# Staging an image's output as two column halves and spreading its stores

## The chip, the cores and the metric

The kernel runs on one core of one Trainium2 chip. The core has a matrix engine (TensorE, PE in the profile), a vector engine (VectorE, DVE), a scalar engine (ScalarE, ACT), GpSimd (POOL) and SyncE (SP), which here only issues transfers. Transfers between device memory and the on-chip memory run on 16 DMA engines, whoever issues them. The metric is the device time of one execution in microseconds, as the median of several runs.

## The reference

The input `x` has 16 images of 64 channels, 128 x 128 pixels, float32. Layer 0 is a spectral convolution: a Hartley transform, a product over channels for the 20 x 20 lowest modes, the inverse transform, a Gaussian blur along all four axes (also batch and channel), and a mask that keeps the columns 0 to 32 and 96 to 127. Layer 1 is a small network on top:

```
h    = afno(group_norm(x)) + x          # spectral mixing of 32 x 32 modes, two small complex layers
feats = gelu(fe_w @ group_norm(h))
out  = mean over 2 shared of gelu(shared_w[s] @ feats)
gate = softmax of the 4 best of 16 expert scores, from the mean of feats, one set per image
out += sum over the 4 chosen experts of gate[e] * gelu(expert_w[e] @ feats)
out += h
```

All products with 64 x 64 weights are per pixel. The output has the size of the input, 4.19 MB per image.

## The kernel before

The first stages transform all images to modes, mix channels, and run the spectral layer; they leave per image 1 MB of column spectra in device memory (`bmd`), further mode tables (`od`, `obd`, `ond`) and a small edge correction (`ehd`). The change doesn't touch them, apart from tables that depend on the order of tiles.

The last stage makes the output, image after image. An image's pixels lie in eight tiles `t` of 16 columns each; the tuple `TILES` (line 32) says which columns the tile `t` holds. A tile has 128 partitions (64 channels times two halves of the rows) and 1024 elements each, so that one matmul group, one Gelu and one vector operation handle it.

The work of an image is cut in pieces (`PIECES`, line 965), each with places counted in groups from the image's first group; an image has `NG` = 48 groups, and all pieces of all images are sorted by place (line 978). The pieces are:

- `spectrum` (line 698), at -84 and -76: SyncE loads the edge correction and four 256 KB slices of `bmd` into the tile `bm`, and then four loads from `od`, `obd`, `ond`. There is one `bm`; a load into it has to wait until TensorE has read the image before.
- `columns` (710), `pixels` (724) and `feature` (796): inverse transforms on TensorE, evacuated by ScalarE (tiles in `BY_ACT`) or VectorE; `pixels` adds the edge correction to the first rows of the tiles that hold columns with a mask of one; `feature` is the first Gelu layer.
- `gate` (816), in eight steps at -3 to 15: the expert scores; its seventh step, at group 12, computes a power on GpSimd (line 869) and issues four gathers (`indirect_dma_start`, line 876) that fetch the four chosen experts' weights into `wl`.
- `group` (947), at 0 to 47: groups 0 to 15 apply the shared weights to the tiles in pairs, groups 16 to 47 the four gathered experts: tiles 0 and 1 for the experts 0 to 3, then 2 and 3, and so on. Each is a product on TensorE, a Gelu on ScalarE (line 901) and an addition on VectorE (line 905). For the last expert the addition writes the result to the staging tile `stg` instead (line 911).
- `stores` (932), at 50 to 66: 17 stores of an image from `stg` to the output, one per group, beside the next image's groups.

TensorE, ScalarE and VectorE run in the order in which the program is written (`in_order`, line 976). Work on ScalarE and VectorE is written one piece late (`on_act`, `on_dve`, `done`), and `flush` writes out what is pending. SyncE isn't in that set: the order of its issues is chosen by a scheduler. Each store gets a dependence on the newest Gelu (`newest`), which paces it. SyncE's transfers use eight semaphores in turn, so that one waits for the transfer eight before it. `stg` has one buffer, so that the additions that write it for one image wait for the stores of the image before. The last image has no next one, and is stored in four quarters of 32 columns as its pairs of tiles are done (line 914).

Of the kernel before, what the change touches and what calls it, by code (L numbers as in the profile page):

```python
# [11 lines left out]
F32 = mybir.dt.float32  # L12
# [6 lines left out]
NB, C, N = 16, 64, 128  # L19
# [9 lines left out]

KR = 116  # L30
EC = 65
TILES = (0, 1, 6, 7, 2, 3, 4, 5)
BY_ACT = (0, 2, 4, 6)
CL = C // 2
NSL = 8
# [21 lines left out]
def constant_tables():  # L57
    th = 2 * np.pi / N
    n, k20, m32 = np.arange(N), np.arange(K), np.arange(MD)
# [18 lines left out]
    e = np.exp(1j * th * np.outer(n, np.arange(K + 1)))  # L78
# [14 lines left out]
    e_cols = np.concatenate([np.stack([s_[:32].reshape(4, 8) for s_ in sides], 1).ravel(), [32]])  # L93
    d1 = e1 - g1 * e
    edge = np.zeros((K, K, 2, EC * 4))
    for k2 in range(K):
# [47 lines left out]
    for k1 in range(K):  # L144
# [35 lines left out]
def hartley_afno_moe_kernel(ctx: ExitStack, tc: tile.TileContext, a: dict, out: bass.AP):  # L180
    nc = tc.nc
    P = 128
# [26 lines left out]
    with tc.tile_pool(name="modes", bufs=1) as mp:  # L209
# [6 lines left out]
        with tc.tile_pool(name="f_x", bufs=10) as xp, tc.tile_pool(name="f_t", bufs=2) as tp, \  # L216
# [70 lines left out]
        with tc.tile_pool(name="m_o", bufs=1) as op, tc.tile_pool(name="m_w", bufs=4) as wp, \  # L287
# [16 lines left out]
            edge = load(sc, "edge", [CH, 4, 2 * EC * 4])  # L304
# [359 lines left out]
    with s3:  # L664
# [59 lines left out]
        def pixels(box, t):  # L724


            if t == 0:
                if box["columns"] < 4:
                    flush()
                box["h"] = []  # L730
            ps = ps2.tile([P, 2, 512], F32, name="pe")
            for j in range(8):
                for s, half in ((0, 0), (1, 1), (0, 1), (1, 0)):
                    rs = slice(s * C, (s + 1) * C)
                    nc.tensor.matmul(ps[half * C:(half + 1) * C, s, j * C:(j + 1) * C],  # L735
                                     lhsT=u[rs, t * 8 + j], rhs=inv2[rs, half], start=True, stop=True)

            def evacuate():
                h = hpp.tile([P, 2, 512], F32, name="h")
                box["h"].append(h)  # L740
                hv = h.rearrange("p s (i m) -> p (s i) m", m=16)
                pv = ps.rearrange("p s (j i) -> p i (s j)", i=C)
                nm = min(16, EC - 16 * t)
                at = 4 if t < 4 and t not in BY_ACT else 0
                if t in BY_ACT:
                    nc.scalar.copy(hv, pv)
                else:
                    nc.vector.tensor_copy(hv[:, at:], pv[:, at:])
                if nm > 0:
                    nc.vector.tensor_tensor(hv[:, 0:4, 0:nm], (pv if at else hv)[:, 0:4, 0:nm],  # L750
                                            box["edge"][:, 64 * t:64 * t + 4 * nm]
                                            .rearrange("p (i m) -> p i m", m=nm), ALU.add)

            on_act(evacuate)
# [134 lines left out]
        def expert(box, t, w, bias, share, last=False):  # L889
            if box["features"] <= t:  # L890
                flush()
            f, h = box["f"][t], box["h"][t]
            ps = ps2.tile([P, 2, 512], F32, name="pe")
            for p, half in ((0, 0), (1, 1), (0, 1), (1, 0)):
                rows_ = slice(p * C, (p + 1) * C)
                nc.tensor.matmul(ps[half * C:(half + 1) * C, p], lhsT=w[rows_],  # L896
                                 rhs=f[rows_, half], start=True, stop=True)

            def activate():
                g = gp.tile([P, 2, 512], F32, name="g")  # L900
                newest[0] = nc.scalar.activation(g, ps, AF.Gelu, bias=bias)  # L901

                def add():
                    if not last:
                        nc.vector.scalar_tensor_tensor(h, g, share(), h, ALU.mult, ALU.add)  # L905
                        return
                    if t == 0:
                        box["out"] = stgp.tile([P, C, N], F32, name="stg")
                    c0 = 16 * TILES[t]
                    gv, hv = (v.rearrange("p s (i m) -> p (s i) m", m=16) for v in (g, h))  # L910
                    nc.vector.scalar_tensor_tensor(box["out"][:, :, c0:c0 + 16], gv, share(), hv,  # L911
                                                   ALU.mult, ALU.add)
                    box["whole"] = t == NSL - 1
                    if box["b"] == NB - 1 and t % 2:
                        for n in range(0, 17, 2):
                            store(box, (n, n + 1), slice(16 * TILES[t - 1], c0 + 16))

                on_dve(add)

            on_act(activate)  # L920

        STORES = [(half, i0 + r, n0 + r, min(8, nr - r))
                  for half, i0, n0, nr in ((0, 0, 0, 64), (1, 4, 64, 60), (1, 0, 124, 4)) for r in range(0, nr, 8)]

        def store(box, ns, cols=slice(0, N)):
            half, i0, n0, e = STORES[ns[0]]
            if len(ns) > 1 and ns[1] < len(STORES) and STORES[ns[1]][2] == n0 + e and n0 + e != 124:
                e += STORES[ns[1]][3]
            return nc.sync.dma_start(out[box["b"], :, n0:n0 + e, cols],
                                     box["out"][half * C:(half + 1) * C, i0:i0 + e, cols])  # L930

        def stores(box, i):
            if box["b"] == NB - 1:
                return
            if not box["whole"]:
                flush()
            tc.add_manual_dep(store(box, (i,)).ins, newest[0].ins.name,
                              mybir.DependencyInfo(mybir.DependencyClass.Sync, mybir.DependencyReason.SCHED_ONLY),
                              reason="an image's store goes out beside the next image's groups")

# [15 lines left out]
        def step(name, make):  # L956
# [6 lines left out]


        PIECES = (
            (stores, tuple(range(NG + 2, NG + 19))),
            (spectrum, (-84, -76)),
            (columns, (-54, -51, -45, -39)),
            (feature, (-34, -27, -20, -20, -15, -14, -8, -4)),
# [2 lines left out]
            (group, range(NG)),  # L972
        )
        norms = norm2()
        boxes = [{"b": b, "whole": False} for b in range(NB)]
# [82 lines left out]
```

## Time and profile before

| | |
|---|---|
| median of 7 runs | 1681.18 us (1676.06 to 1685.38) |
| the profiled execution | 1679.41 us, its span 1677.6 us |
| mean granted TensorE clock | 0.968 |
| TensorE busy | 1525.4 us, 91% |
| ScalarE busy | 1273.1 us, 76% |
| VectorE busy | 1268.2 us, 76% |
| GpSimd busy | 152.6 us, 9% |
| q1, the transfers of SyncE | 172790 packets, 193.76 MB, 46.0% of 16 engines |

The span is cut in 40 slices of 42 us, whose digits are the busy share of an engine in tenths. Waits are listed by the instruction that waited and what released it, with their sum, their number and the longest. In a list in order of time each row has its start, its length, engine, line, operation, output<-input and the idle time before it in brackets. Rows of stretches have, for each engine, the busy time and the number of instructions, then the granted TensorE clock (1.00 is full), the busy share of the DMA engines and GB/s. The landing time of a transfer runs from the start of its issue until its semaphore tells that it is complete.

### The profile page before, as it was taken

The page shows a single profiled execution, that of the slowest core. Times are in us where ns is not written, and L with a number is a line of the kernel's source. Part 1 is how long each engine was busy: PE and PEld are TensorE (multiplying, and loading weights), DVE is VectorE, ACT ScalarE, POOL GpSimd, SP SyncE. Part 2 cuts the span into 40 slices and gives each one's busy share as a digit, 9 for nine tenths or more (in the row PEclk, how much of TensorE's full clock was granted, in tenths as well). Part 3 has the DMA queues.
Part 4 walks back from the last instruction along what each step waited for, and adds up shares of the span by engine and source line. Part 5 has one row for each costly group of instructions (what it writes and reads, how often), then busy time and mean ns, then how long its engine had stood idle before and what let it go on. Part 6 is the DMA issues. An engine that isn't in the chain of part 4 may idle for free.

```text
span 1677.6 us, 62043 instructions
## 1 busy us (share of the span) xinstructions
PE 1525.4 (91%) x27656; PEld 817.0 (49%) x27656; DVE 1268.2 (76%) x1700; ACT 1273.1 (76%) x1631; POOL 152.6 (9%) x152
## 2 busy tenths in 40 slices
PE   6787858799997999999999999999999999999984
PEld 6777745233334545444454444544445445454420
DVE  0344434356664599998999989999899998999986
ACT  2233334155565899998999989999899999999975
POOL 0000002000122101011010110101101011011020
PEclk9999979899997999999999999999999999999987
DMA  9889964443575206245162360633606336154046
GB/s 386 308 298 312 315 151 118 109 114 86 122 172 148 44 15 133 65 85 130 24 134 70 78 136 22 131 80 67 138 20 132 85 62 138 31 117 88 20 104 101
DMA packets 177521, 205.09 MB, mean 122 GB/s; under 512 B 129178, under 2 KB 134278, under 8 KB 174878
## 3 DMA queue, kind: packets, MB, share of 16 engines
q1 hardware_dynamic: 172790, 193.76, 46.0%
q0 software_dynamic: 4464, 7.35, 1.7%
q8 instruction: 218, 3.57, 0.9%
q14 instruction: 49, 0.40, 0.1%
HBM read 109.86 MB, written 91.20 MB: 120 GB/s over the span
## 4 chain that ended last, share of the span: by engine, by line
PE 72%; issue 10%; DMA 7%; ACT 5%; DVE 3%; SPq 1%; POOL 1%; POOLq 0%; DVEq 0%; ACTq 0%
PE pe L896 32%; PE pe L715 7%; PE psx L638 7%; PE ps L272 7%; PE pe L735 5%; PE pe L806 5%; DMA wl<-exd,ati 4%; ACT g L901 3%; PE ps L232 3%; PE psd L560 2%; DMA spec_sb<-in_spec_dram 1%; PE psd L539 1%; PE pso L586 1%; PE pso L574 1%; DMA edge_sb<-in_edge_dram 1%
## 5 line engine op out<-in xcount | busy, mean ns | idle before, releaser
L901 ACT ACTIVATE g<-pe,wl 128x1024 f32<-128x1024 f32 x512 | 553.4, 1207 | 32.0 <-PE pe L896 29.6
L896 PE MATMUL pe<-f,wl 64*64 64x512 f32 x4096 | 493.8, 603 | 27.0 <-DMA wl<-exd,ati 24.4
L905 DVE SCALAR_TENSOR_TENSOR h<-g,wt,h 128x1024 f32<-128x1024 f32 x384 | 472.9, 1281 | 34.7 <-ACT g L901 33.7
L905 DVE SCALAR_TENSOR_TENSOR h<-g,h 128x1024 f32<-128x1024 f32 x256 | 301.3, 1218 | 13.1 <-ACT g L901 13.1
L901 ACT ACTIVATE g<-pe,vec_sb 128x1024 f32<-128x1024 f32 x256 | 269.0, 1115 | 10.9 <-PE pe L896 10.8
L896 PEld LDWEIGHTS pe<-f,wl 64*64 64x64 f32 x4096 | 147.4, 135 | 253.6 <-issue 136.5
L896 PE MATMUL pe<-f,shw 64*64 64x512 f32 x2048 | 244.3, 595 | 0.5 <-DVE ati L872 0.3
L272 PE MATMUL ps<-fwd_sb,xt 128*64 128x64 f32 x4096 | 155.6, 232 | 36.3 <-issue 29.1
L735 PEld LDWEIGHTS pe<-inv_sb,u 64*64 64x64 f32 x8192 | 149.3, 136 | 64.8 <-issue 37.6
L275 ACT COPY t<-ps 128x320 f32<-128x320 f32 x128 | 53.8, 426 | 146.9 <-PE ps L272 146.6
L272 PEld LDWEIGHTS ps<-fwd_sb,xt 128*64 128x64 f32 x4096 | 144.1, 146 | 42.8 <-issue 35.2
L911 DVE SCALAR_TENSOR_TENSOR stg<-g,wt,h 128x1024 f32<-128x1024 f32 x128 | 158.5, 1281 | 1.3 <-DVE h L750 0.8
L810 ACT ACTIVATE f<-pe,fba 128x1024 f32<-128x1024 f32 x128 | 154.4, 1216 | 2.9 <-PE pe L806 2.9
L715 PEld LDWEIGHTS pe<-inv_sb,bm 116*64 116x64 f32 x4096 | 129.3, 142 | 52.7 <-ACT g L901 34.9
L735 PE MATMUL pe<-inv_sb,u 64*64 64x64 f32 x8192 | 152.6, 221 | 2.2 <-ACT u L719 1.1
L715 PE MATMUL pe<-inv_sb,bm 116*64 116x64 f32 x4096 | 138.2, 228 | 2.1 <-issue 1.3
L806 PE MATMUL pe<-h,fsa 64*64 64x512 f32 x1024 | 131.8, 590 | 2.0 <-DVE h L750 2.0
L638 PE MATMUL psx<-spec_sb,ot 100*32 100x512 f32 x1024 | 117.9, 602 | 9.6 <-DMA spec_sb<-in_spec_dram 9.6
L241 DVE TENSOR_TENSOR xm<-ps,pn 64x20 f32<-64x20 f32 x32 | 5.5, 171 | 158.0 <-ACT pn L237 157.7
L869 POOL TENSOR_TENSOR dv<-root_e,dv 128x4 f32<-128x4 f32 x16 | 34.6, 2163 | 963.8 <-DVE ati L872 857.2
L896 PEld LDWEIGHTS pe<-f,shw 64*64 64x64 f32 x2048 | 71.5, 133 | 99.4 <-issue 70.0
L232 PE MATMUL ps<-fwd_sb,t 128*64 128x64 f32 x1280 | 62.4, 230 | 21.5 <-issue 12.7
(186 smaller groups left out, 1259.2 us busy)
## 6 DMA issues: line engine op xcount, KB each, us to landing
xt<-in_x_dram SPq DMA_DIRECT2D x128, 512.0 KB
out_dram<-stg SPq DMA_DIRECT2D x225, 256.0 KB
bmd<-bs SPq DMA_DIRECT2D x32, 512.0 KB
bm<-bmd SPq DMA_DIRECT2D x64, 256.0 KB
out_dram<-stg SPq DMA_DIRECT2D x58, 128.0 KB
wk<-in_w_dram SPq DMA_DIRECT2D x11, 320.0 KB
wn<-in_w_dram SPq DMA_DIRECT2D x11, 320.0 KB
spec_sb<-in_spec_dram SPq DMA_DIRECT2D x1, 3200.0 KB
```

The source lines that it names most:

```text
L232: nc.tensor.matmul(ps[h * C:(h + 1) * C, m, :], lhsT=t1[:, j, :], rhs=fwd2[:, j, :], start=(t == 0), stop=(t == 1))
L272: nc.tensor.matmul(ps[cols, i, :], lhsT=xt[:, i, cols], rhs=fwd1, start=True, stop=True)
L275: nc.scalar.copy(t1[:, :, c0:c0 + 8], src)
L638: nc.tensor.matmul(ps[p0:p0 + CL], lhsT=ot[:, kc, b * C + h * CL:b * C + (h + 1) * CL], rhs=spec[:, kc, ri * 1024 + n * 512:ri * 1024 + (n ...
L715: nc.tensor.matmul(ps[s * C:(s + 1) * C, i // 8, i % 8], lhsT=bm[0:KR, 16 * q + i], rhs=inv1[0:KR, s], start=True, stop=True)
L735: nc.tensor.matmul(ps[half * C:(half + 1) * C, s, j * C:(j + 1) * C], lhsT=u[rs, t * 8 + j], rhs=inv2[rs, half], start=True, stop=True)
L806: nc.tensor.matmul(ps[p * C:(p + 1) * C, half], lhsT=fsa[rows_, box["b"]], rhs=box["h"][t][rows_, p], start=True, stop=True)
L810: nc.scalar.activation(f, ps, AF.Gelu, bias=fba[:, box["b"]:box["b"] + 1], accum_out=box["sums"][:, t:t + 1])
L896: nc.tensor.matmul(ps[half * C:(half + 1) * C, p], lhsT=w[rows_], rhs=f[rows_, half], start=True, stop=True)
L901: newest[0] = nc.scalar.activation(g, ps, AF.Gelu, bias=bias)
L905: nc.vector.scalar_tensor_tensor(h, g, share(), h, ALU.mult, ALU.add)
L911: nc.vector.scalar_tensor_tensor(box["out"][:, :, c0:c0 + 16], gv, share(), hv, ALU.mult, ALU.add)
```

## The change

The order of tiles becomes (0, 1, 2, 3, 6, 7, 4, 5): the tiles 0 to 3 now hold the columns 0 to 63, the tiles 4 to 7 the columns 64 to 127. The tiles with a non-zero edge correction are now 0, 1, 4, 5 and, with one column, 2 (`EDGED`). The staging tile of 128 x 64 x 128 elements becomes two of 128 x 64 x 64, `stg0` for the left and `stg1` for the right half, each with a buffer of its own.

An image's stores become nine per half: seven of 16 rows, one of 12 and one of 4. A row of a store is 64 columns, 256 bytes, in the output, where a row of the output has 512 bytes; before, a store held whole rows, eight of them in a run of 4 KB. The left half's stores stand at 34 to 58, in the image's own groups, the right half's at 60 to 80, beside the next image's groups 12 to 32. SyncE joins the engines whose order is that of the source.

The last image is stored as its left half at once, and then in two quarters of 32 columns.

```diff
-TILES = (0, 1, 6, 7, 2, 3, 4, 5)
+TILES = (0, 1, 2, 3, 6, 7, 4, 5)
+EDGED = {0: (0, 16), 1: (64, 16), 4: (128, 16), 5: (192, 16), 2: (256, 1)}
...
-                nm = min(16, EC - 16 * t)
-                at = 4 if t < 4 and t not in BY_ACT else 0
+                e0, nm = EDGED.get(t, (0, 0))
+                at = 4 if nm > 1 and t not in BY_ACT else 0
...
-                                            box["edge"][:, 64 * t:64 * t + 4 * nm]
+                                            box["edge"][:, e0:e0 + 4 * nm]
...
-                    if t == 0:
-                        box["out"] = stgp.tile([P, C, N], F32, name="stg")
-                    c0 = 16 * TILES[t]
+                    if t % 4 == 0:
+                        box["out"].append(stgp.tile([P, C, C], F32, name=f"stg{t // 4}"))
+                    c0 = 16 * TILES[t] % C
...
-                    nc.vector.scalar_tensor_tensor(box["out"][:, :, c0:c0 + 16], gv, share(), hv,
+                    nc.vector.scalar_tensor_tensor(box["out"][-1][:, :, c0:c0 + 16], gv, share(), hv,
                                                    ALU.mult, ALU.add)
-                    box["whole"] = t == NSL - 1
-                    if box["b"] == NB - 1 and t % 2:
-                        for n in range(0, 17, 2):
-                            store(box, (n, n + 1), slice(16 * TILES[t - 1], c0 + 16))
+                    box["staged"] = t + 1
+                    if box["b"] == NB - 1 and t in (3, 5, 7):
+                        for n in range(9):
+                            store(box, t // 4, n, slice(0, C) if t == 3 else slice(c0 - 16, c0 + 16))
...
+        def store(box, g, n, cols):
+            half, i0, n0, e = STORES[n]
+            return nc.sync.dma_start(out[box["b"], :, n0:n0 + e, g * C + cols.start:g * C + cols.stop],
+                                     box["out"][g][half * C:(half + 1) * C, i0:i0 + e, cols])
...
-            if not box["whole"]:
+            g, n = divmod(i, 9)
+            if box["staged"] < 4 * g + 4:
                 flush()
...
-            (stores, tuple(range(NG + 2, NG + 19))),
+            (stores, (34, 37, 40, 43, 46, 49, 52, 55, 58, 60, 62, 65, 67, 70, 72, 75, 77, 80)),
...
-        in_order = {mybir.EngineType.PE, mybir.EngineType.Activation, mybir.EngineType.DVE}
+        in_order = {mybir.EngineType.PE, mybir.EngineType.Activation, mybir.EngineType.DVE,
+                    mybir.EngineType.SP}
```

More of the change, by code (lines that the diff above doesn't have):

```diff
@@ L92, in constant_tables @@
             inv2[r:r + 32, j], inv2[r + 32:r + 64, j] = np.cos(a32)[:, ns], -np.sin(a32)[:, ns]
-    e_cols = np.concatenate([np.stack([s_[:32].reshape(4, 8) for s_ in sides], 1).ravel(), [32]])
+    e_cols = np.concatenate([s_[8 * t:8 * t + 8] for t, (_, m) in EDGED.items() if m > 1 for s_ in sides] + [[32]])
     d1 = e1 - g1 * e
@@ L906, in add @@
                         return
-                    if t == 0:
-                        box["out"] = stgp.tile([P, C, N], F32, name="stg")
-                    c0 = 16 * TILES[t]
+                    if t % 4 == 0:
+                        box["out"].append(stgp.tile([P, C, C], F32, name=f"stg{t // 4}"))
+                    c0 = 16 * TILES[t] % C
                     gv, hv = (v.rearrange("p s (i m) -> p (s i) m", m=16) for v in (g, h))
-                    nc.vector.scalar_tensor_tensor(box["out"][:, :, c0:c0 + 16], gv, share(), hv,
+                    nc.vector.scalar_tensor_tensor(box["out"][-1][:, :, c0:c0 + 16], gv, share(), hv,
                                                    ALU.mult, ALU.add)
-                    box["whole"] = t == NSL - 1
-                    if box["b"] == NB - 1 and t % 2:
-                        for n in range(0, 17, 2):
-                            store(box, (n, n + 1), slice(16 * TILES[t - 1], c0 + 16))
+                    box["staged"] = t + 1
+                    if box["b"] == NB - 1 and t in (3, 5, 7):
+                        for n in range(9):
+                            store(box, t // 4, n, slice(0, C) if t == 3 else slice(c0 - 16, c0 + 16))
                 on_dve(add)
             on_act(activate)
[L922 to L930, printed above, removed]
+        STORES = [(half, i0 + r, n0 + r, min(16, nr - r))
+                  for half, i0, n0, nr in ((0, 0, 0, 64), (1, 4, 64, 60), (1, 0, 124, 4)) for r in range(0, nr, 16)]
+        def store(box, g, n, cols):
+            half, i0, n0, e = STORES[n]
+            return nc.sync.dma_start(out[box["b"], :, n0:n0 + e, g * C + cols.start:g * C + cols.stop],
+                                     box["out"][g][half * C:(half + 1) * C, i0:i0 + e, cols])
         def stores(box, i):
@@ L934, in stores @@
                 return
-            if not box["whole"]:
+            g, n = divmod(i, 9)
+            if box["staged"] < 4 * g + 4:
                 flush()
-            tc.add_manual_dep(store(box, (i,)).ins, newest[0].ins.name,
+            tc.add_manual_dep(store(box, g, n, slice(0, C)).ins, newest[0].ins.name,
                               mybir.DependencyInfo(mybir.DependencyClass.Sync, mybir.DependencyReason.SCHED_ONLY),
-                              reason="an image's store goes out beside the next image's groups")
+                              reason="an image's store goes out beside other images' groups")
         GROUPS = [(t, k) for shared, nk in ((True, 2), (False, TOPK)) for t0 in range(0, NSL, 2)
@@ L974, in hartley_afno_moe_kernel @@
         norms = norm2()
-        boxes = [{"b": b, "whole": False} for b in range(NB)]
-        in_order = {mybir.EngineType.PE, mybir.EngineType.Activation, mybir.EngineType.DVE}
+        boxes = [{"b": b, "staged": 0, "out": []} for b in range(NB)]
+        in_order = {mybir.EngineType.PE, mybir.EngineType.Activation, mybir.EngineType.DVE,
+                    mybir.EngineType.SP}
         with tc.manual_schedule(engines=in_order):
```

## The prediction

> **What bounds the kernel now.** I read the page's head and slices first, then what TensorE waited for, then one image's gather in order of time, then stretches with the granted clock and the DMA share.
>
> ```profile
> span 1677.6 us, 62043 instructions
> PE   6787858799997999999999999999999999999984
> ACT  2233334155565899998999989999899999999975
> DMA  9889964443575206245162360633606336154046
> ```
> From slice 13 on, sixteen images pass, one per 68 us. TensorE and ScalarE are both near 9; the 16 DMA engines alternate between 6 and 0 inside each image. The stores of an image come as one burst.
>
> ```profile
> core 0: us, PE busy (x) PEld busy (x) DVE busy (x) ACT busy (x) POOL busy (x), PEclk, DMA share, GB/s
> 1005.00:1074.00 69.00, 68.25 (x1240) 33.92 (x1236) 64.50 (x72) 66.03 (x77) 6.34 (x5) 0.99 0.38 84
> ```
> One image: TensorE 68.3 of 69 us, ScalarE 66.0, VectorE 64.5. Only TensorE's own losses can be won, and only until ScalarE (about 66) ends the image.
>
> ```profile
> PE pe L896 <- DMA wl<-exd,ati: 24.4, 15, 6.1
> PE pe L896 <- ACT g L901: 2.5, 2, 1.3
> ```
> This list of TensorE's waits shows the one steady loss in that stage: the first expert matmul of each image (group 16) waits for its gathered weights. 24.4 less the last image's 6.1 is 18.3 us; the two waits put down to ScalarE (1.3 and 1.2) stand at the same place in images 5 and 11, so the loss is 20.8 us over images 0 to 14, 1.4 us each.
>
> ```profile
> 1203.40 1.23 POOL L876 DMA_INDIRECT wl<-exd,ati  x1 [0.19 <-ACT g L901]
> 1207.47 2.30 SPq L929 DMA_DIRECT2D out_dram<-stg  x1
> 1209.71 1.09 PE L896 MATMUL pe<-f,wl 64*64 64x512 f32 x8 [2.59 <-DMA wl<-exd,ati]
> 1210.86 1.11 ACT L901 ACTIVATE g<-pe,wl 128x1024 f32<-128x1024 f32 x1 [2.59 <-PE pe L896]
> ```
> Image 9: the gather is issued at 1203.40 and TensorE starts on it 6.3 us later, after idling 2.59; ScalarE idles with it. TensorE was ready at 1207.12, 3.7 us after the issue; in image 7 it was 3.4. So a gather that lands within 3.4 us costs nothing. The gathers' landing times (least, median, most) are:
>
> ```profile
> DMA to landing us min/median/max: 2.3/4.3/6.4
> ```
> The stretches around it show why it is late, and what a long wait does afterwards:
>
> ```profile
> 1203.00:1207.00 4.00, 3.98 (x90) 1.85 (x80) 3.87 (x7) 3.49 (x5) 3.20 (x4) 1.00 0.99 206
> 1207.00:1210.00 3.00, 0.41 (x8) 0.24 (x8) 3.00 (x4) 1.11 (x1) 1.31 (x2) 1.00 0.93 194
> 1210.00:1213.00 3.00, 3.00 (x80) 2.05 (x76) 0.17 (x1) 1.88 (x2) 0.00 (x0) 0.68 0.95 139
> 1213.00:1216.00 3.00, 3.00 (x27) 1.13 (x23) 2.34 (x3) 2.14 (x3) 0.00 (x0) 0.75 0.49 97
> 1216.00:1219.00 3.00, 3.00 (x88) 1.81 (x84) 3.00 (x4) 3.00 (x4) 0.00 (x0) 1.00 0.09 10
> ```
> While the gather flies the DMA engines are 0.93 to 0.99 busy with stores; ten microseconds later they stand at 0.09. After the 2.59 us wait the granted clock (column before the DMA share) is 0.68 and 0.75 for 6 us: 3 x 0.32 + 3 x 0.25 = 1.7 us more. Images 3 and 6 (waits of 2.5 and 2.4) run 71.4 and 71.1 us to the next gather, by the issue times in the chain, where the others run 68 to 69; after waits of 1.5 and less the clock stays 1.00.
>
> **The change, part by part.** The order of instructions on TensorE, ScalarE, VectorE and GpSimd in the built program is the one of before. On VectorE the edge additions go to other tiles in equal numbers and sizes, and the staging write keeps its 1024 elements (1281 ns each): nothing. Its staging write now waits for DMA semaphores twice per image instead of once, up to 8 more waits at the 17 ns of a semaphore event in SyncE's list, 0.14 us of VectorE's 4 idle us per image: nothing, and if that cover were gone 15 x 0.14 = 2 us.
>
> *The stores.* 17 of mostly 256 KB become 18; the rows written fall from 4 KB runs to 256 B runs. The trace has no 256 B store. Its bounds are the 4 KB stores, 213 GB/s at 0.99 busy (stretch 1067 to 1071), and the 128 B stores of the last image:
>
> ```profile
> 1637.00:1647.00 10.00, 10.00 (x84) 2.08 (x80) 10.00 (x10) 10.00 (x11) 0.00 (x0) 1.00 0.80 103
> 1647.00:1653.00 6.00, 6.00 (x52) 1.25 (x48) 6.00 (x6) 6.00 (x7) 0.00 (x0) 1.00 1.06 174
> 1656.00:1662.00 6.00, 0.00 (x0) 0.00 (x0) 6.00 (x6) 1.67 (x2) 0.00 (x0) 0.69 1.01 169
> 1666.00:1676.00 10.00, 0.00 (x0) 0.00 (x0) 0.00 (x0) 0.00 (x0) 0.00 (x0) 0.50 0.81 103
> ```
> Two quarters move at 103 GB/s, two at about 170. An image's 4.19 MB takes 19.7 us at 213 and 40.7 at 103; I take 150, 28 us, in the middle of the near rows. The DMA engines stand idle 0.62 x 68 = 42 us per image, so 8 us more (21 at worst) hides. SyncE issues a store of 1024 runs as quickly as before (median 0.67 us), and one goes out per 2.5 to 3 groups, 3.5 to 4.3 us, against 1.75 us to move it (2.5 at worst): no backlog.
>
> [...]
>
> *SyncE in the source's order.* Before, loads of the spectrum for the next image but one stood between the stores, each held by TensorE's reads of `bm`; SyncE waited 22.6 us for one of them in image 7 and then sent 17 stores from 1051 to 1077. Now stores wait only for ScalarE's place in the order. Following the semaphore values of the built program to ScalarE's and TensorE's times in this trace, image 7 would have: store at 1061.7, `edge` and four `bm` loads to 1064.7, stores at 1065.3 and 1070.2. Its gather was issued at 1067.06 and out of GpSimd at 1068.3. What is queued then is 0.26 + 0.13 + 1.05 + 0.26 = 1.7 MB from 1062.5, at 213 GB/s done about 1070.5, instead of a queue full until 1078. The `od`, `obd` and `ond` loads follow at 1075 to 1077; the columns that need them start at group 42, some 30 us later, so a delay there is hidden.
>
> *The gather's landing* is the disputed price. Bounds: 2.3 us (least) and the 4.8 of now (mean of the first gathers' steps in the chain, 4.0 to 6.4). Nearest is a queue running out: image 14's second and third gathers, issued while the stores end (share 0.79), landed in 3.3 us. I take 3.3. With TensorE ready after 3.4 to 3.7 that leaves about 0.2 us per image for jitter: 14 x 0.2 = 2.8 of the 19.7 us of images 1 to 14. Image 0 has no stores beside it and keeps its 1.1. Gone too are three slow-clock spells, 3 x 1.7 = 5.1, and 0.8 of the last image's 3.5 us landing.
>
> [...]
>
> *What of it becomes time.* 19.7 - 2.8 + 5.1 + 0.8 = 22.8 us of TensorE. ScalarE needs 66 of an image's 68.4 us and would end it at about 67; where it is late next (matmuls waiting for its PSUM reads) part is lost. I count 80%: 18.2.
>
> *The last image.* Its first two quarters (1 MB at 1636 and at 1646) become one half of 2.1 MB at 1646; the third and fourth stay. At 150 GB/s the half runs from 1647 to 1661, the third (6 us) to 1667, the fourth (10.2) to 1677 instead of 1676: +1 us; at 213 nothing, at 103 the end is 1684, +8.
>
> Sum on the profiled execution (1679.4 us, span 1677.6): -18.2 + 1 = -17, so 1662.4. The median of the seven runs is 1.8 us above it: **1664**.
>
> **The rivals.** *The gathers land as late as before*, because the 1.05 MB of spectrum loads now stand at their very group: 1681 + 1 = 1682. For it: 4 KB packets are ahead of them in both programs. Against: the loads are issued 3 us before the gather is ready and nothing is behind them.
>
> *Narrow rows cost the lower bound* (103 GB/s): the last image ends 8 us later, gathers land at 4.0 and leave 0.5 us, 7 of the 19.7: (19.7 - 7 + 5.1) x 0.8 = 14, so 1681 - 14 + 8 = 1675.
>
> *Slower: the gather loses against four loads and two stores started together.* If it lands 0.5 us later than now, 15 x 0.5 = 7.5 us more wait, and some five more images pass the 2.4 us at which the clock falls, 5 x 1.7 = 8.5: 1697; with 1 us, 15 + 10 x 1.7 = 32: 1713. It decides from a landing of about 4.9 us. Against it: 1.7 MB stand in line, not a burst of 4.19. For it: eight DMAs can be outstanding in both programs, and five start within 3.5 us.
>
> **How the numbers follow.** This kernel's runs spread 1676 to 1685, so about 0.3% (5 us) can be told from no change. Chances: forecast 0.62, narrow rows at the bound 0.10 (faster), as late as before 0.13 (the same), slower 0.15. Narrow rows that cost even more than the bound move 0.02 from faster. Faster 0.70, same 0.13, slower 0.17. The forecast's own range: everything won (19.7 + 5.1 + 0.8 = 25.6) gives 1655; landing 4.0, 70% of it, +4 at the end gives 1673. The range of 8 in 10 is 1653 to 1688, which takes in the same-as-before case and the mildest of the slower one.
>
> **What would show it.** Right: TensorE's wait for `wl` at the expert matmul near 1.1 + 3 us outside the last image; landing median near 3.3; DMA slices evenly 4 to 6; no granted clock below 0.9 between 660 and 1550; images of about 67 us; 256 B packets. Wrong: landings still over 4 us, VectorE waiting for DMA before the staging write, columns waiting for `bm`, or stores running on more than 3 us longer after VectorE's last write.

## The result, and the profile after

The changed kernel takes 1704.44 us (median, 1689.75 to 1713.52) where the kernel before took 1682.67 us beside it: a ratio of 1.013, 95% interval 1.0113 to 1.0147. It is slower by 1.3%. The prediction said 1664 us, faster, and the time lies above its range of 1653 to 1688.

The head and slices of the changed kernel's page, and the line of SyncE's queue:

```profile
span 1696.9 us, 62072 instructions
...
PEclk9999979899996999999999999999999999999997
DMA  9888865344475224555555655555454565545447
...
q1 hardware_dynamic: 394134, 193.76, 53.4%
```

The stores are spread as the change says: from slice 15 on (counted from 0, the last one apart) the DMA digits stand evenly at 4 to 6, where they went from 0 to 6 before. The bytes are the same, the packets more than twice as many, and the queue's share rose from 46.0% to 53.4%. None of this ends an image. The wait that does is in the list of waits (sum, times, longest):

```profile
PE pe L897 <- DMA wl<-exd,ati: 39.2, 17, 5.5
```

Before, the same line read 24.4, with 6.1 in the last image. So TensorE's wait for the gathered weights, which the change was predicted to remove, went from 18 to 34 us outside the last image. The landing times of the gathers (least, median, most; 2.3, 4.3, 6.4 before) have risen too. In both kernels the trace tells them for the second to fourth gather of each image only, 48 of 64; the first gather, for which TensorE waits, is not among them:

```profile
DMA to landing us min/median/max: 2.5/5.3/6.9
```

From the gather of image 1 to that of image 15 the time is 984.2 us instead of 966.9, 17.3 more. TensorE's idle time ahead of the first expert matmul of images 1 to 14 is 13.5 us more (32.4 instead of 18.9), and slow clocks cost 4.2 us more: the 100 matmuls after the wait take 5.03 us at the full clock and 6.65 after some of the long waits, and what they take above 5.03 is 10.6 us in all, 6.4 before (of which 0.9 is a second wait, in image 10). The two together are 17.7 us, the 17.3 but for 0.4. Of the other 2.0 us of the span's 19.3, the stretch ahead of the first gather is 3.3 longer (it ends at 587 us instead of 583; over all runs but experiment 8 it ends between 583 and 592, so this says nothing of the change), and the last image is 1.25 shorter.

Image 9 of the changed kernel in order of time, with the rows that matter (SPq is SyncE issuing):

```profile
1215.04 0.60 SPq L928 DMA_DIRECT2D out_dram<-stg  x1
1215.69 0.83 SPq L704 DMA_DIRECT2D edge<-ehd  x1
...
1216.62 2.89 SPq L706 DMA_DIRECT2D bm<-bmd  x4
...
1218.00 1.24 POOL L877 DMA_INDIRECT wl<-exd,ati  x1 [0.19 <-ACT g L902]
...
1219.61 3.68 SPq L928 DMA_DIRECT2D out_dram<-stg  x2
...
1224.57 1.19 PE L897 MATMUL pe<-f,wl 64*64 64x512 f32 x8 [3.09 <-DMA wl<-exd,ati]
```

The four `bm` loads, 1 MB in 4 KB packets, are issued from 1.4 us before the gather until 1.5 us after it, for an image whose columns need them some 40 us later. TensorE starts on the gathered weights 6.57 us after their issue, and has idled 3.09. The same image in stretches (busy time of the engines, granted clock, DMA share, GB/s):

```profile
core 0: us, PE busy (x) PEld busy (x) DVE busy (x) ACT busy (x) POOL busy (x), PEclk, DMA share, GB/s
1214.00:1218.00 4.00, 4.00 (x98) 2.17 (x94) 3.89 (x7) 4.00 (x6) 2.02 (x1) 1.00 0.44 68
1218.00:1222.00 4.00, 3.48 (x88) 1.64 (x80) 3.93 (x7) 3.59 (x5) 3.36 (x3) 1.00 1.03 233
1222.00:1226.00 4.00, 1.43 (x29) 0.96 (x33) 2.68 (x4) 0.83 (x2) 0.94 (x1) 0.93 1.06 229
1226.00:1230.00 4.00, 4.00 (x75) 2.34 (x72) 1.36 (x2) 2.80 (x3) 0.00 (x0) 0.64 0.04 9
```

The DMA engines are less than half busy until the gather is issued, full for the eight microseconds from then on, and idle (0.04) right after. The granted clock falls to 0.64 behind the wait.

### The profile page after: what moved, and what is told of

Read it like the earlier page. It is cut to its first block, busy times and chain, and to the rows that moved or that the text cites. A ratio compares the mean times of both kernels' runs of the same rounds, so it can differ in the third digit from the quotient of the medians.

```text
span 1696.9 us, 62072 instructions
## 1 busy us (share of the span) xinstructions
PE 1526.9 (90%) x27656; PEld 815.1 (48%) x27656; DVE 1267.5 (75%) x1700; ACT 1274.5 (75%) x1631; POOL 153.7 (9%) x152
## 3 DMA queue, kind: packets, MB, share of 16 engines
q1 hardware_dynamic: 394134, 193.76, 53.4%
## 4 chain that ended last, share of the span: by engine, by line
PE 68%; issue 11%; DMA 9%; ACT 5%; DVE 4%; SPq 1%; POOL 1%; DVEq 0%; POOLq 0%; ACTq 0%
PE pe L897 30%; PE pe L716 7%; PE ps L273 6%; PE psx L639 6%; PE pe L736 5%; PE pe L807 5%; DMA wl<-exd,ati 5%; ACT g L902 3%; PE ps L233 2%; DMA spec_sb<-in_spec_dram 1%; PE psd L561 1%; DVE h L906 1%; PE psd L540 1%; PE pso L587 1%; DMA fwd_sb<-in_fwd_dram 1%
## 5 line engine op out<-in xcount | busy, mean ns | idle before, releaser
L906 DVE SCALAR_TENSOR_TENSOR h<-g,wt,h 128x1024 f32<-128x1024 f32 x384 | 472.7, 1281 | 33.6 <-ACT g L902 32.4
L906 DVE SCALAR_TENSOR_TENSOR h<-g,h 128x1024 f32<-128x1024 f32 x256 | 301.0, 1217 | 13.1 <-ACT g L902 13.1
L736 PEld LDWEIGHTS pe<-inv_sb,u 64*64 64x64 f32 x8192 | 153.0, 140 | 68.0 <-issue 41.2
L749 DVE COPY h<-pe 128x960 f32<-128x960 f32 x64 | 76.0, 1187 | 8.2 <-PE pe L736 8.1
```

## The experiments

The theory after reading the trace, called A in the expectations, is that SyncE's new order puts the spectrum loads on the gather. The first rival, B, is that the narrow rows of the stores delay it. A later one, F, is TensorE's own instruction fetches. The table sums up all runs. "Loads" is when the first and the last `bm` load are issued, in us from the gather's issue (median over images 1 to 13; negative is earlier); "store" is the issue of the stores from 3 us before to 3 us after it in a usual image; "start" is the mean time from the gather's issue to the first expert matmul, over images 0 to 14; "wait" is TensorE's idle time ahead of it, summed over these images. Loads, stores, starts and waits are from the one profiled execution of each kernel, the median is over its runs, and ratios are to the kernel before on the same chip. Not all rows come from the same chip (the kernel before took 1678 to 1683 us beside them), so rows are best compared by their ratios.

| kernel | loads | store | start | wait | median us | ratio, 95% |
|---|---|---|---|---|---|---|
| before | -27.9, -5.6 | -1.2, -0.6, 0.3, 1.6 | 4.8 | 20.0 | 1682.7 | |
| changed | -1.6, 1.2 | -3.0, 1.6 | 5.7 | 33.5 | 1704.4 | 1.0113 to 1.0147 |
| 1: loads late | 9.9, 12.4 | -3.0, 0.0 | 4.7 | 20.0 | 1680.3 | 0.9956 to 1.0008 |
| 2: scheduler's SyncE | -26.2, -5.9 | -3.0, 0.0 | 4.5 | 15.7 | 1672.7 | 0.9921 to 0.9966 |
| 3: before + SyncE's order | -1.8, 0.8 | -3.0, 1.3, 2.0 | 6.0 | 36.1 | 1709.2 | 1.0129 to 1.0201 |
| 4: no stores | -27.9, -6.3 | none | 4.1 | 11.1 | 1669.2 | 0.9893 to 0.9949 |
| 5: loads late, gap | 8.8, 11.4 | -3.0 | 3.2 | 1.5 | 1658.7 | 0.9830 to 0.9903 |
| 6: before, order, late | 7.2, 9.5 | -3.0, -2.0, 0.0, 1.0 | 3.9 | 6.4 | 1671.5 | 0.9911 to 0.9967 |
| 7: loads early | -5.3, -3.4 | -2.7, 0.0 | 5.3 | 28.2 | 1690.1 | 1.0025 to 1.0077 |
| 8: 1, fetches shifted | 9.8, 12.5 | -3.0, 0.0 | 4.7 | 20.1 | 1692.2 | one run |
| 9: 6 with the gap | 11.0, 13.5 | -3.0 | 3.2 | 1.3 | 1655.9 | 0.9777 to 0.9891 |
| 10: gap only | -1.6, 1.0 | -3.0 | 5.7 | 33.2 | 1704.5 | 1.0075 to 1.0201 |
| 11: loads early, gap | -5.2, -2.7 | -2.0 | 4.7 | 20.0 | 1675.6 | 0.9955 to 0.9992 |

**1. The spectrum loads after the gather.** One line of the changed kernel:

```diff
-            (spectrum, (-84, -76)),
+            (spectrum, (-77, -70)),
```

> The changed kernel with the spectrum loads moved from groups 12 and 20 to groups 19 and 26 (places -77 and -70), behind the gathers. Theory A (the 1.05 MB of spectrum loads, now issued at the gather's own group, delay it): the gathers land in 2.5 to 3.5 us, TensorE waits under 5 us for them over images 1 to 14 instead of 32, time 1660 to 1670. Theory B (the 256 B rows, spread over all groups, delay it): landing stays near 5 us, time 1695 to 1710.

Measured: 1680.3 us, the same as before; the loss is gone with the loads. It is not the gain that A expected, though (1660 to 1670 us, under 5 us of waits): the waits are 20 us, as before the change. Most images wait 0.7 to 1.1 us. What is left is in two parts, seen in images 8 and 9 in order of time:

```profile
1140.16 1.26 POOL L877 DMA_INDIRECT wl<-exd,ati  x1 [0.19 <-ACT g L902]
1140.18 5.09 SPq L928 DMA_DIRECT2D out_dram<-stg  x2
...
1144.42 1.09 PE L897 MATMUL pe<-f,wl 64*64 64x512 f32 x8 [0.93 <-DMA wl<-exd,ati]
```

```profile
1208.11 1.23 POOL L877 DMA_INDIRECT wl<-exd,ati  x1 [0.19 <-ACT g L902]
...
1213.93 1.09 PE L897 MATMUL pe<-f,wl 64*64 64x512 f32 x8 [2.51 <-DMA wl<-exd,ati]
```

In the usual image the store of group 62 is issued with the gather; its 256 B packets fill the DMA engines from 1.2 to 3 us after it, and the gather's first packet starts at 2.4 to 3.0 us (at 2.0 in experiment 5, where nothing is beside it). In images 3, 6, 9 and 12 the wait is 2.3 to 2.6 us with the same stores. That was unexplained at this point; experiments 5 and 8 take it up.

**2. Without SyncE's order.** The columns and the stores' groups stay, SyncE's order goes back to the scheduler:

```diff
-        in_order = {mybir.EngineType.PE, mybir.EngineType.Activation, mybir.EngineType.DVE,
-                    mybir.EngineType.SP}
+        in_order = {mybir.EngineType.PE, mybir.EngineType.Activation, mybir.EngineType.DVE}
```

> The changed kernel with SyncE out of the ordered engines again: halves and spread stores stay, the scheduler puts the bm loads right behind TensorE's reads, some groups before the gather, and the od loads near it. Theory A: the 4 KB loads are mostly through when the gather starts; landing 3 to 4 us, time 1665 to 1682. Theory B: landing near 5 us, 1695 to 1710.

Measured: 1672.7 us, 0.6% faster than before. The scheduler sends the `bm` loads one by one between the stores, the last 5.9 us ahead of the gather. So the halves and the spread stores without SyncE's order are a small gain; the one edit of the order costs some 32 us against this version (1704.4 to 1672.7, and as much by the ratios).

**3. SyncE's order alone, in the kernel before.** The edit of experiment 2 the other way round, on the kernel before, with whole rows of 4 KB runs and the 17 stores at groups 50 to 66.

> The kernel before with SyncE added to the ordered engines, nothing else: whole-row stores at groups 2 to 18 of the next image, spectrum loads among them at groups 12 and 20. Theory A: the gather meets stores and loads together; landing 5 us or more, time 1695 to 1720. Theory B: whole rows, so it stays as before, 1676 to 1690.

Measured: 1709.2 us, with the waits even longer than in the changed kernel:

```profile
PE pe L896 <- DMA wl<-exd,ati: 41.2, 15, 6.2
```

With no narrow row in an image's store, SyncE's order alone makes the whole loss. B is rejected as its cause.

**4. No stores.**

```diff
         def stores(box, i):
-            if box["b"] == NB - 1:
-                return
+            return
```

> The changed kernel without the stores of images 0 to 14 (their output is left out); the last image is stored. Theory A: the loads are still at the gather; landing 4 to 5 us, TensorE waits 10 to 25 us over images 1 to 14, time 1675 to 1695. Theory B: nothing narrow is left beside the gather; landing 2.5 to 3 us, waits under 3 us, time 1655 to 1665.

Measured: 1669.2 us, outside both ranges. A's premise did not hold: without stores to pace it SyncE ran ahead, and the `bm` loads were issued 28 to 6 us ahead of the gather instead of at it. Outside the last image no wait is longer than 1.1 us, but most images still wait 0.7 to 1.0. The short loads from `od`, `obd` and `ond` (80 B packets) were still running when the gather flew; that they make these waits was not tested by itself. Removing every store gains less than moving stores and loads (experiment 5), so it is not the amount of data in all that counts.

**5. Loads late, and a gap in the stores.** Experiment 1, and no store between groups 60 and 65:

```diff
-            (stores, (34, 37, 40, 43, 46, 49, 52, 55, 58, 60, 62, 65, 67, 70, 72, 75, 77, 80)),
-            (spectrum, (-84, -76)),
+            (stores, (34, 37, 40, 43, 46, 49, 52, 54, 56, 58, 60, 65, 67, 69, 72, 74, 77, 80)),
+            (spectrum, (-77, -70)),
```

> The changed kernel with the spectrum loads at the groups of the first experiment, and with the stores' groups moved so that none lies at the gather: one store less between group 60 and group 65. Theory A (what flies beside the gather delays it): with nothing but the end of the store of group 60 in flight, the gather's first packets start 2.0 to 2.4 us after its issue (2.0 with no stores, 2.95 in the first experiment's usual image), TensorE starts its first expert matmul at +3.2 to +3.6, the waits of images 0 to 14 fall from 20.0 us in all to 6 to 10, no image waits over 1.9 us and the slow-clock stretches go: 20 - 8 = 12 us less of waits and some 4 us of clock, 1662 to 1668 us, ratio to before 0.988 to 0.992. Rival R (the gather costs 3.5 us whatever flies, and the first experiment's 20 us is a floor): 1678 to 1683 us. Rival F (the waits of every third image come from something that is not on the store's queue, such as TensorE's own instruction fetches of 16 KB): the usual images' waits go, but images 3, 6, 9 and 12 still wait over 2 us: sum 10 to 13 us, 1670 to 1674 us.

Measured: 1658.7 us, below what A expected. Image 9 in order of time, and in stretches:

```profile
1190.03 8.06 SPq L928 DMA_DIRECT2D out_dram<-stg  x2
...
1193.00 1.23 POOL L877 DMA_INDIRECT wl<-exd,ati  x1 [0.19 <-ACT g L902]
...
1196.09 1.07 PE L897 MATMUL pe<-f,wl 64*64 64x512 f32 x8
```

```profile
core 0: us, PE busy (x) PEld busy (x) DVE busy (x) ACT busy (x) POOL busy (x), PEclk, DMA share, GB/s
1193.00:1197.00 4.00, 4.00 (x99) 2.15 (x93) 3.93 (x7) 3.74 (x5) 3.36 (x3) 1.00 0.08 22
```

The expert matmul carries no bracket any more: TensorE comes to it at about 3.1 us without having idled. The DMA engines stand at 0.08 where they stood at 1.03, and the four microseconds are full of TensorE work. The waits of the images 1 to 13 are gone, and so are the drops of the clock after them; these images take 66.9 to 67.8 us each instead of 67.8 to 71.6. Rival R (a floor) is rejected. F expected images 3, 6, 9 and 12 to stay late in this kernel; they do not. TensorE is busy for 66.89 of the 66.9 us of image 8, ScalarE for 65.6. What becomes of F is left to experiment 8.

**6. The kernel before with SyncE's order and late loads.**

> The kernel before with SyncE in the source's order and the spectrum loads at the later groups: whole 4 KB rows, stores at their old groups 50 to 66, no loads beside the gather. Theory A: as the first experiment, 1676 to 1684 us, waits of images 0 to 14 of 18 to 24 us. Theory B (narrow rows cost the changed kernel something besides): below the first experiment by 5 us or more, 1670 to 1675. Third case (stores in whole rows at groups 58 to 64 delay the gather more than narrow ones, as they run faster and closer together): 1686 to 1694.

Measured: 1671.5 us, in the range that was given to B, and below experiment 1 by 9 us (7 by the ratios). Here four stores lie beside the gather, more than in experiment 1, and yet all images but 0 and 3 wait 0.04 to 0.8 us. The row of a stretch below is from image 9, whose gather is issued at 1206.24:

```profile
PE pe L896 <- DMA wl<-exd,ati: 10.8, 7, 6.1
```

```profile
core 0: us, PE busy (x) PEld busy (x) DVE busy (x) ACT busy (x) POOL busy (x), PEclk, DMA share, GB/s
1206.00:1210.00 4.00, 3.90 (x92) 1.99 (x88) 3.93 (x7) 3.58 (x6) 3.20 (x4) 1.00 0.94 205
```

The DMA engines are as full (0.94) as in the kernel before (0.93 to 0.99), and this image waits 0.07 us. So busy DMA engines alone do not make a gather late. Why these paced stores of whole rows hurt so little, where the kernel before with four stores of the same kind beside its gather waits 20 us, is not shown.

Beside experiment 1 it also suggests that narrow rows have a price, if a smaller one than the loads: there hardly any of the gather's packets starts until the narrow store's packets are through (the first at 2.9 us after the issue in the mean), here they start among the 4 KB packets at 2.3. The stores' places differ too, so this is an argument and not shown.

**7. Loads two groups earlier.**

```diff
-            (spectrum, (-84, -76)),
+            (spectrum, (-86, -76)),
```

> The changed kernel with edge and the four spectrum loads two groups earlier (10 instead of 12), ahead of the store of group 60: about 2.8 us earlier on SyncE, which is nearly where the prediction had placed them. Theory A with the place as the failed step: the loads' packets end about 2.4 us after the gather's issue instead of 5.2, TensorE starts at +4.2 to +4.8 instead of +5.5, the waits of images 0 to 14 come to 18 to 24 us instead of 33.5, and the time to 1682 to 1690 us. If the prediction's own premise holds once the loads stand where it put them: 1660 to 1668. If the place of the loads within these 2.8 us does not matter: 1700 to 1708.

Measured: 1690.1 us, at the upper end of A's range in time and beyond it in waits (28.2). Moving the loads by some 4 us, ahead of a store, gives back 14 of the 24 us that moving them away gives. Image 8, where they come a microsecond later than in most images:

```profile
1135.98 1.48 SPq L704 DMA_DIRECT2D edge<-ehd  x1
1137.56 2.43 SPq L706 DMA_DIRECT2D bm<-bmd  x4
1140.08 6.97 SPq L928 DMA_DIRECT2D out_dram<-stg  x3
1141.93 1.27 POOL L877 DMA_INDIRECT wl<-exd,ati  x1 [0.19 <-ACT g L902]
...
1148.14 1.13 PE L897 MATMUL pe<-f,wl 64*64 64x512 f32 x4 [2.87 <-DMA wl<-exd,ati]
```

**8. TensorE's instruction fetches moved by a third.** Experiment 1 with, ahead of the image loop:

```diff
         with tc.manual_schedule(engines=in_order):
+            z = few_columns()
+            for _ in range(43):
+                nc.tensor.matmul(z[:, 0:1], lhsT=grp, rhs=grp[:, 0:1], start=True, stop=True)
```

> The first experiment with 43 one-column matmuls (86 instructions) put ahead of TensorE's instructions of the last stage; nothing of the image loop is changed. TensorE's instructions come in 16 KB packets about every 256 instructions, and an image takes about nine and two thirds of these. Rival F (the fetch beside the gather makes the images 3, 6, 9 and 12 of the first experiment wait 2.3 to 2.6 us): with a third of a fetch more ahead of the loop the long waits move to the images 1, 4, 7, 10 and 13 (or 2, 5, 8, 11, 14), and 3, 6, 9 and 12 wait 0.8 to 1.1. If the pattern comes from anything else (buffers in turn, SyncE's places), the long waits stay at 3, 6, 9 and 12. The time itself tells little: the first experiment's 1680 plus 3 to 9 us for the added matmuls.

Measured: the long waits moved to the images 2, 5, 8, 11 and 14 (2.4, 2.1, 2.5, 2.4, 2.5 us); 3, 6, 9 and 12 wait 0.7 to 0.8. Images 8 and 9 in order of time:

```profile
1148.26 1.27 POOL L877 DMA_INDIRECT wl<-exd,ati  x1 [0.19 <-ACT g L902]
...
1154.11 1.14 PE L897 MATMUL pe<-f,wl 64*64 64x512 f32 x8 [2.51 <-DMA wl<-exd,ati]
```

```profile
1219.40 1.23 POOL L877 DMA_INDIRECT wl<-exd,ati  x1 [0.19 <-ACT g L902]
...
1223.38 1.09 PE L897 MATMUL pe<-f,wl 64*64 64x512 f32 x8 [0.67 <-DMA wl<-exd,ati]
```

Nothing in the loop was touched except the phase of the fetches, so the pattern is theirs. The DMA rows of experiment 1 show one 16 KB packet of the instruction queue per fetch, 218 in all; in images 3, 6, 9 and 12 it starts 3.3 to 3.6 us after the gather, and TensorE starts 1.2 to 1.3 us after it has ended. In the stretch 1211.2 to 1212.8 of image 9 it is all but alone with the gathers (eight last packets of SyncE's queue aside):

```profile
q0 software_dynamic: 59, 0.06, 16.7%
q8 instruction: 1, 0.02, 4.1%
```

It runs from 1211.71 to 1212.77, and one of the gathers' 4 B packets (16 to a gather in the changed kernel's trace) starts at 1212.76. In image 9 of the changed kernel the first gather's last 4 B packet starts 5.38 us after the issue, 0.88 behind the one before it, and a fetch runs from 3.95 to 5.40. That this packet waited behind the fetch on one DMA engine fits, but the trace does not name the engine. TensorE did not simply run out of instructions: in experiment 2, image 6, it started 0.2 us before such a fetch was over. In the kernel before, the same fetch stands beside the long waits of images 3, 6 and 9 (from 3.5 to 4.0 until 4.7 to 5.1 us after the gather's issue). In experiment 5 the first gather's packets are through at 2.2 to 2.5 us, the fetch in images 3, 6, 9 and 12 starts at 2.3 us or later, and F's pattern disappears. The one image there that waits beside image 0 and the last is 14 (0.43 us), and there a fetch runs from 1.6 to 2.6 us, across the gather's packets. In experiment 6 the images 2, 5, 8, 11 and 14, with a fetch between 1.0 and 2.3 us, wait 0.4 to 0.8 us, and the others but 0 and 3 at most 0.11. So a fetch can cost something without a late gather. The time of the run (13 us more ahead of the first gather, for the added matmuls among others) says nothing.

**9. Experiment 6 with a gap: no column halves.**

```diff
-            (stores, tuple(range(NG + 2, NG + 19))),
-            (spectrum, (-84, -76)),
+            (stores, tuple(range(50, 61)) + (65, 65, 66, 66, 67, 67)),
+            (spectrum, (-77, -70)),
...
-        in_order = {mybir.EngineType.PE, mybir.EngineType.Activation, mybir.EngineType.DVE}
+        in_order = {mybir.EngineType.PE, mybir.EngineType.Activation, mybir.EngineType.DVE,
+                    mybir.EngineType.SP}
```

> The kernel before (one staging buffer, whole 4 KB rows, 17 stores) with SyncE in the source's order, the spectrum loads at the later groups, and no store between group 60 and group 65: the quiet stretch at the gather without the two column halves. If the quiet stretch is all that the gain of the fifth experiment needs (theory A alone): waits of images 0 to 14 below 5 us, 1656 to 1664 us, the same as the fifth experiment within its interval. If the halves are needed, because the last stores at groups 65 to 67 keep the one staging buffer from the next image's first writes near group 70: VectorE waits there for a transfer, 1666 to 1680 us.

Measured: 1655.9 us, 1.7% below the kernel before and the fastest of all, though not to be told from experiment 5. One staging buffer, whole rows and a burst of stores are no hindrance here, with the gather in a quiet stretch. In image 10 (the gather is issued at 1259.60) the burst is on until 1259, at 0.83, and then stops:

```profile
core 0: us, PE busy (x) PEld busy (x) DVE busy (x) ACT busy (x) POOL busy (x), PEclk, DMA share, GB/s
1255.00:1259.00 4.00, 4.00 (x94) 2.00 (x90) 3.89 (x7) 4.00 (x5) 1.60 (x1) 1.00 0.83 199
1259.00:1263.00 4.00, 4.00 (x96) 2.30 (x96) 3.93 (x7) 3.72 (x6) 3.20 (x4) 1.00 0.16 35
```

**10. The gap alone.** The changed kernel with the stores' groups of experiment 5, the loads where they were.

> The changed kernel with the stores' groups of the fifth experiment alone: the spectrum loads stay at group 12 of the gather. Theory A with the loads as the main part of the delay: their 1 MB in 4 KB packets still flies from 1 us before to 5 us after the gather's issue, TensorE starts at +4.8 to +5.5, the waits come to 25 to 31 us and the time to 1690 to 1699 us. If the narrow store of group 62 were the main part: waits of 12 to 18 us and 1672 to 1682 us. If the two only hurt together: 1658 to 1668 us.

Measured: 1704.5 us, no change that these four runs can tell, a miss for all three cases; the waits came to 33.2 us where A said 25 to 31:

```profile
PE pe L897 <- DMA wl<-exd,ati: 38.8, 15, 5.6
```

As long as the loads lie on the gather, the store that follows them costs nothing more. With the loads gone, the same edit is worth some 20 us (experiment 1 to 5). The two are no sum.

**11. Loads early, and the gap.** Experiments 7 and 10 together; this is the queue that the prediction had in mind.

> The changed kernel with the spectrum loads at group 10 (as in the seventh experiment) and no store between groups 60 and 65 (as in the fifth): the loads stand where the prediction put them (issued 5.2 to 3.4 us ahead of the gather), and what follows them is the store of group 60 alone, instead of two. The prediction's landing of 3.3 us, from a queue that runs out in time: waits of 2 to 6 us in all, 1660 to 1668. If the loads alone, even issued so early, still hold the gather back (1.3 MB in line, at 213 GB/s done 1 to 2 us after the gather's issue, and the short runs of 80 B that follow): TensorE starts at +4 to +4.8, waits 10 to 20 us, 1672 to 1682. If the store of group 62 made no difference in the seventh experiment: 1686 to 1694.

Measured: 1675.6 us, in the middle case. TensorE starts 4.7 us after the gather's issue in the mean, no clock is lost, and the waits are 20.0 us, as many as before the change. Image 8 in order of time, and the line of the waits:

```profile
1130.53 0.60 SPq L928 DMA_DIRECT2D out_dram<-stg  x1
...
1131.93 3.07 SPq L706 DMA_DIRECT2D bm<-bmd  x4
...
1135.09 7.23 SPq L928 DMA_DIRECT2D out_dram<-stg  x2
...
1137.12 1.27 POOL L877 DMA_INDIRECT wl<-exd,ati  x1 [0.19 <-ACT g L902]
...
1141.84 1.09 PE L897 MATMUL pe<-f,wl 64*64 64x512 f32 x8 [1.33 <-DMA wl<-exd,ati]
```

```profile
PE pe L897 <- DMA wl<-exd,ati: 25.4, 15, 5.4
```

Here the last 4 KB packet runs until 2.3 us after the gather's issue, the store of group 60 behind it until 3.2.

## Why the prediction was wrong

**The bound was right.** TensorE's wait for the gathered weights, plus the slow clock after it, is what could be won: in experiment 5 these fell by 18.4 and 6.1 us, and the stretch from image 1 to image 15 by 26.4. The share that becomes time was taken as 80%; it was all of it, and ScalarE did not become the bound (65.6 us of an image's 66.9).

**The stores were right.** Where the last image's left half fills the DMA engines, its 256 B packets move at 160 GB/s (predicted 150):

```profile
1668.00:1678.00 10.00, 6.00 (x48) 1.13 (x48) 10.00 (x10) 8.88 (x9) 0.00 (x0) 0.90 1.02 160
```

The DMA digits are even, VectorE waits 0.5 us in all for a transfer before it writes a staging tile, and no column waits for `bm`. The last image's +1 us came out as nothing: its stores end 13.0 us after VectorE's last write, 13.1 before. That the image is 1.25 us shorter comes from its shorter wait for the gather (0.55) and slow clock after it (1.1).

**The step that failed first is the place of SyncE's loads.** The prediction put the store, `edge` and the four `bm` loads 5.3 to 2.4 us ahead of the gather. The trace has the store 3.0 us ahead of it, and the loads from 1.4 us before to 1.5 us after it. Two readings were off. In the changed kernel the store goes out 0.03 us after a Gelu that ends 3.0 us ahead of the gather. The kernel before has the Gelus in the same places: in image 7 three of them end 4.0, 3.0 and 2.0 us ahead of the gather at 1067.06. What ends at the predicted 1061.7 is a copy on ScalarE ahead of them:

```profile
1060.72 1.01 ACT L719 COPY u<-pe 128x1024 f32<-128x1024 f32 x1 [0.29 <-PE pe L715]
1061.95 3.12 ACT L901 ACTIVATE g<-pe,vec_sb 128x1024 f32<-128x1024 f32 x3 [0.22 <-PE pe L896]
```

And store, `edge` and the four loads take SyncE 4.5 us to issue (1215.04 to 1219.51 in image 9), not 3.0. With loads and stores near the prediction's places (experiment 11) the time is 1675.6 instead of 1704.4, 26 to 29 us less (by ratios and by medians); with the loads alone moved (experiment 7) it is 14 us less. The store moved away with them is no part of this by itself (experiment 10).

**The second is the gather's landing of 3.3 us.** Even from that place TensorE could start only after 4.7 us, not 3.3 to 3.7, and the waits were 20.0 us instead of 3.9 (2.8, and image 0's 1.1). The 3.3 was taken from the second and third gathers of an image whose stores were ending; the first gather decides, and in experiment 11, behind a queue that ends 2 to 3 us after its issue, TensorE starts after 4.3 to 5.6 us (images 0 to 13). The saving of 17 us becomes the 3.3 that experiment 11 measured.

**The rival that came about** is the slower one: loads and stores started together with the gather. Its price for 0.5 us later (1697) and for 1 us later (1713) encloses the measured 0.9 us later on average (5.7 instead of 4.8) and 1704. Its clock term was too large: three more images lost the clock (six instead of three), not five to ten. Against it the prediction said that 1.7 MB in line is less than a burst of 4.19. That was the wrong measure: with loads and narrow stores in line, the wait went not with how much was queued but with whether it was over when the gather's first packet could start, about 2 us after its issue (2.0 in experiment 5). The rival that gathers land as late as before did not happen.

**The clock** was right as a term. After the changed kernel's waits of 1.9 to 3.8 us the 100 matmuls took 6.3 to 7.6 us in six images, and 5.0 to 5.5 in the others, some of them after waits of 1.9 to 2.6. So no length of wait separates the two: image 6 lost the clock after 1.86 us, image 1 kept it after 2.60.

## What to carry to other kernels

A small transfer on the critical path can pay for what else is in flight in the few microseconds between its issue and its landing, and not all traffic costs the same: here TensorE started 3.1 us after the gather's issue in quiet (experiment 5), mostly 3.5 to 4.2 beside paced stores of whole rows (experiment 6), 4.0 to 4.4 beside a narrow store where no fetch came in between (experiment 1), and 5.7 in the mean beside 1 MB of loads. Place the bulk transfers around it, in time and not only in the order of issue, and read that place from the trace to within a microsecond: here 4 us in the place of the loads were worth 14 us, and 26 to 29 with the store behind them moved too. An engine's order written by hand brings that duty with it: where a scheduler had spread the loads, the source's order sent them in one burst at the very place where they were written. And once a wait is known to depend on a short stretch, the cheapest experiment is to empty this stretch before anything is rebuilt; here it beat both kernels with a few edited numbers.

## What was not expected

- TensorE's instruction fetch is a transfer too. Its 16 KB packets take 0.9 to 1.5 us each in the changed kernel and come about every 256 instructions (55312 instructions of PE and PEld in 217 packets there, 255 to a packet); where one falls on the end of a gather, TensorE starts some 1.5 us later (5.6 to 5.9 us after the gather's issue in experiment 1, against 4.0 to 4.4). An image has about nine and two thirds of them (some 2480 instructions), so the pattern repeats every third image.
- A slow clock does not follow every wait. In experiment 1 the 100 matmuls after the waits of 2.57, 2.29 and 2.54 us took 6.6 us, after the one of 2.51 us 5.03. What decides it is not shown.
- Loads from `od`, `obd` and `ond` in runs of 80 B keep DMA engines busy for longer than their bytes suggest: in experiment 4 some 60 such packets per 0.5 us were still running 6 us after the gather, at a share of about 0.1, and gathers landed in 3.9 us (median) instead of the 2.8 of experiment 5; that these packets are the cause is not shown.
- The 128 B rows of the last image's stores do not all run at one rate. In the kernel before, the columns 0 to 31 and 64 to 95 go at 103 GB/s, the columns 96 to 127 and 32 to 63 at 174 and 169 (the rows in the prediction); in the changed kernel 64 to 95 go at 107 and 96 to 127 at 179. It is the place of the columns, not the order of writing, that goes with the rate; why is not shown.
